# Due times of row tails, and half norms on VectorE, in a graph attention kernel

## The chip, the cores and the metric

The kernel runs on one core of one Trainium2 chip. The metric is the time of one execution on the device in microseconds (us). All times below are in microseconds unless marked otherwise. The engines are TensorE (PE in the profile; PEld is its weight load), VectorE (DVE), ScalarE (ACT), GpSimd (POOL) and SyncE (SP, which only issues transfers here). Each engine runs its own instructions in order and waits on semaphores for the others.

## The reference

Eight graphs (F) of 2048 nodes (N) with 256 channels (C) share one 0/1 adjacency matrix. Each gets masked attention with eight heads of 32 channels, a normalisation, a two-layer network, a second normalisation, and around the whole a residual and a third normalisation. All is float32.

```
qkv = einsum('fnc,ck->fnk', x, w_qkv)                  # q, k, v, 8 heads of 32
scores = einsum('fnhd,fmhd->fhnm', q, k) / sqrt(D)
scores = where(adj > 0, scores, -1e9)
t = einsum('fhnm,fmhd->fnhd', softmax(scores), v)
x1 = layernorm(x + t) * ln1_g + ln1_b
f_out = relu(x1 @ w1 + b1) @ w2 + b2
x2 = layernorm(x1 + f_out) * ln2_g + ln2_b
out = layernorm(x + x2)                                # no gain, no bias
```

`layernorm` subtracts the row's mean and divides by sqrt(variance + 1e-5).

## The kernel before

**Items.** `fast_path` walks 1024 items (f, qc, g, mb): graph f, chunk qc of 512 query rows (four a graph), group g of four heads (two), block mb of 128 keys (sixteen). So a chunk is 32 items and a graph 128. For one item `scores` issues the score matmuls of four heads into two PSUM pairs and two VectorE additions of the mask (L279) into a tile `p`; `exponentials` is one ScalarE activation over 128x2048 (L283); `values` multiplies with V and accumulates over the sixteen blocks (L310); `add_up` adds up the exponentials for the softmax denominators, some on GpSimd (L339), some by transfers that accumulate (L336). Scores run two items ahead of the values, and three PSUM pairs take turns. There are twelve `p` tiles. The very last half chunk (`ENDING`, the last chunk's second head group) is computed in two halves of 256 rows, with lines of its own (L264, L268, L298, L330, L332).

**Side work.** Everything else is written as generators: projections of the next graph (`project`, `ask`, `turn`), mask blocks, and for each chunk, when its 32 items are done, `denominator` (L383 to L398), `outcome` with `divide` (transposes, division by the denominators, and a transfer L418 that accumulates `x` into `y`), and `tail`. A tail is: `norm` of `y`; `feed_forward` (transposes of `y`, two layers on TensorE, GpSimd's scale L581 and shift L583 of the residual); `norm` again; GpSimd's scale L445 and shift L447; a transfer L450 that adds `x`; a third `norm`; the store L453. `norm` takes statistics on VectorE (L348, L349), computes 1/sqrt on GpSimd (L353 to L357) and applies it on ScalarE (L360). Each `yield n` hands back to the planner for n steps.

**The planner.** In every step `advance` first runs side work, then the step's exponential, scores and values are issued. Generators stand in a list sorted by their due time, the third argument of `start`; those that want a PSUM bank (`yield BANK`) go in that order as long as a budget of TensorE work a step (`credit`) lasts, or at once when one of them is due. A larger due time therefore puts a generator behind others. What the planner decides is fixed when the program is built; nothing is chosen at run time.

**Due times.** `outcome` starts a chunk's tail ten steps after its `begin`, due at `begin + 26`. Two chunks are special: chunk 1 of the last graph has `begin + 18` and two rows at a time (`per` 2), and chunk 2 of the last graph, which gets its residual from a tile `xb` through TensorE, starts at `begin + 4` and is due at `begin + 18`.

**The end.** The last chunk is finished by `closing(h)`, once for each half of 256 rows: five matmul terms of the denominators (L494) and their sum with the first head group's (L497), transposes, division (L526), residual (L529), statistics (`half_stats`, L460 to L464, 1/sqrt on GpSimd), `half_norm` (a small VectorE product L469 and two ScalarE activations L471), GpSimd's scale and shift L535 and L536, the two layers, and the two remaining norms with L559, L564 and L565 between them, then the store L569. When the items are out, `advance` runs what is left in the order of due times; half 1 has the earlier due time.

Of the kernel before, what the change touches and what calls it, by code (L numbers as in the profile page):

```python
# [61 lines left out]
def fast_path(ctx, tc, cst, x, adj, out, RS):  # L62
# [339 lines left out]
    def outcome(f, qc):  # L402
        yield ROOM
        state["tails"] += 1
        xin = x[f, qc * CH:(qc + 1) * CH, :].rearrange("(p j) c -> p j c", p=P)
        y = yp.tile([P, TPC, C], F32, name="y")
        begin = items.index((f, qc, 1, LAST)) + SUM + 2
        yield from divide(f, qc, y)
        if (f, qc) == (F - 1, NCK - 2):
            xb = state["xb"]  # L410
            for j in range(0, TPC, 2):
                yield BANK
                ps = bank()
                columns(ps, ident, xb[:, j:j + 2, :].rearrange("p j c -> p (j c)"), start=True, stop=True)
                nc.vector.tensor_tensor(y[:, j:j + 2, :], ps.rearrange("p (j c) -> p j c", c=C), y[:, j:j + 2, :], ALU.add)
            start(begin + 4, tail(f, qc, y, xin, 2, xb), begin + 18)
            return
        nc.gpsimd.dma_start(y, xin, accum_op=ALU.add)  # L418
        if (f, qc) == (F - 1, NCK - 3):
            start(begin + 10, tail(f, qc, y, xin, 2), begin + 18)  # L420
        else:
            start(begin + 10, tail(f, qc, y, xin), begin + 26)

    def divide(f, qc, y):
        rc = RC.pop((f, qc))
# [9 lines left out]
    def tail(f, qc, y, xin, per=1, xb=None):  # L435
        yield from norm(y, per)
        yield from feed_forward(y)
        if xb is not None:
            nc.gpsimd.tensor_tensor(xb, xb, rows(cst["be2r"]), ALU.add)
        yield 1  # L440
        z = y
        yield from norm(z, per if per == 1 else TPC)
        while xb is None and per > 1 and state["now"] % MB not in CALM:
            yield 1
        nc.gpsimd.tensor_tensor(z, z, rows(cst["g2r"]), ALU.mult)  # L445
        yield 1
        nc.gpsimd.tensor_tensor(z, z, rows(cst["be2r"]) if xb is None else xb, ALU.add)  # L447
        yield 1
        if xb is None:
            nc.gpsimd.dma_start(z, xin, accum_op=ALU.add)  # L450
            yield 7 if per == 1 else 10
        yield from norm(z, per)
        nc.sync.dma_start(out[f, qc * CH:(qc + 1) * CH, :].rearrange("(p j) c -> p j c", p=P), z)  # L453
        state["tails"] -= 1

    def half_stats(t):
        mv = small.tile([P, 2, nc.vector.BN_AGGR_DIM], F32, name="mv")
        for j in range(2):
            st = small.tile([P, nc.vector.BN_STATS_DIM], F32, name="st")
            nc.vector.bn_stats(st, t[:, j, :])  # L460
            nc.vector.bn_aggr(mv[:, j, :], st)
        rs = small.tile([P, 2], F32, name="rs")
        nc.gpsimd.tensor_scalar(rs, mv[:, :, 1], EPS, 1.0, op0=ALU.add, op1=ALU.mult)
        nc.gpsimd.tensor_tensor(rs, rs, cst["mhalf"][:, 0:2], ALU.pow)  # L464
        return mv, rs

    def half_norm(t, mv, rs):
        nb = small.tile([P, 2], F32, name="nb")
        nc.vector.scalar_tensor_tensor(nb, mv[:, :, 0], -1.0, rs, op0=ALU.mult, op1=ALU.mult)  # L469
        for j in range(2):  # L470
            nc.scalar.activation(t[:, j, :], t[:, j, :], AF.Identity, bias=nb[:, j:j + 1], scale=rs[:, j:j + 1])  # L471

    def closing(h):
        f, qc, g = ENDING
        own, part, t0 = slice(2 * h, 2 * h + 2), slice(h * HQ, (h + 1) * HQ), len(items) - MB // 2 * (2 - h)
        terms = [(5, 6), (1, 7), (0, 7), (6, 8), (7, 8)]
        dst = out[f, qc * CH + h * HQ:qc * CH + (h + 1) * HQ, :].rearrange("(p j) c -> p j c", p=P)

        def row2(v):
            return v[:, None, :].to_broadcast([P, 2, C])  # L480

        yield BANK
        ps = bank()
        for n, (block, when) in enumerate(terms):
            if n:
                yield MORE
            while state["now"] < t0 + when:
                yield WAIT
            term = PT.pop((*ENDING, block + h * MB // 2))
            state["credit"] -= 4 * CH  # L490
            for b in range(2):
                for i in range(4):
                    r = D * i
                    nc.tensor.matmul(ps[r:r + D, 0:HQ], cst["halves"][:, g, :], term[:, i, b * HQ:(b + 1) * HQ],  # L494
                                     start=(n + b == 0), stop=(n + b == len(terms)))
        dT = DT[f, qc]
        nc.vector.tensor_tensor(dT[:, part], ps[:, 0:HQ], dT[:, part], ALU.add)  # L497
        if h == 0:
            state["y"] = yp.tile([P, TPC, C], F32, name="y")
            state["ff"] = [work.tile([P, 2, CH], F32, name=n) for n in ("turned", "hT")]  # L500
        y, (yT, hT) = state["y"][:, own], state["ff"]
        xr, xb = (t[:, own] for t in state["rows"])
        def turned_sums():
            ps = bank()
            transposes(ps, [dT[:, part][:, j::2] for j in range(2)])
            den = ps[:, 0:HQ].rearrange("p (j c) -> p j c", c=P)[:, :, ::D // 2]
            rc = op.tile([P, 2, H], F32, name="rc")
            nc.vector.reciprocal(rc, den)
            return rc, den

        def count(den):
            nc.vector.tensor_tensor(RS[:, 0, own], RS[:, 0, own], den, ALU.add)
            nc.vector.tensor_tensor(RS[:, 1, own], RS[:, 1, own], den, ALU.min)

        yield 1
        if h == 0:
            yield BANK
            rc, den = turned_sums()
            count(den)
        yield BANK  # L520
        po = bank()
        transposes(po, [OT[f, qc, gg][:, part][:, j::2] for gg in range(2) for j in range(2)])
        if h:
            rc, den = turned_sums()
        for gg in range(2):
            nc.vector.tensor_tensor(y[:, :, gg * P:(gg + 1) * P].rearrange("p j (h d) -> p j h d", d=D),  # L526
                                    po[:, gg * HQ:(gg + 1) * HQ].rearrange("p (j h d) -> p j h d", h=4, d=D),
                                    rc[:, :, gg::2, None].to_broadcast([P, 2, 4, D]), ALU.mult)
        nc.vector.tensor_tensor(y, y, xr, ALU.add)  # L529
        found = half_stats(y)  # L530
        if h:
            count(den)
        yield 1
        half_norm(y, *found)
        nc.gpsimd.tensor_tensor(xr, y, row2(cst["g1r"]), ALU.mult)  # L535
        nc.gpsimd.tensor_tensor(xr, xr, row2(cst["be1b2r"]), ALU.add)  # L536
        yield BANK
        ps = bank()
        transposes(ps, [y[:, j, a * P:(a + 1) * P] for a in range(2) for j in range(2)])
        for a in range(2):  # L540
            nc.scalar.activation(yT[:, a, part], ps[:, a * HQ:(a + 1) * HQ], AF.Identity,
                                 bias=cst["be1c"][:, a:a + 1], scale=cst["g1c"][:, a:a + 1])
        yield 1
        for d in range(2):
            yield BANK
            ps = bank()
            for a in range(2):
                columns(ps[:, 0:HQ], w1s[:, a, d * P:(d + 1) * P], yT[:, a, part], start=(a == 0), stop=(a == 1))
            nc.scalar.activation(hT[:, d, part], ps[:, 0:HQ], AF.Relu, bias=cst["b1s"][:, d:d + 1], scale=1.0)
        yield 1  # L550
        yield BANK
        ps = bank()
        for j in range(2):
            if j:
                yield MORE
            for d in range(2):
                columns(ps[:, j * C:(j + 1) * C], hT[:, d, part][:, j * P:(j + 1) * P], w2s[:, d, :], start=(d == 0), stop=(d == 1))
        z = y
        nc.vector.tensor_tensor(z, ps.rearrange("p (b c) -> p b c", c=C), xr, ALU.add)  # L559
        found = half_stats(z)  # L560
        yield 1
        half_norm(z, *found)
        yield 1
        nc.vector.tensor_tensor(z, z, row2(cst["g2r"]), ALU.mult)  # L564
        nc.vector.tensor_tensor(z, z, xb, ALU.add)  # L565
        found = half_stats(z)
        yield 1
        half_norm(z, *found)
        nc.sync.dma_start(dst, z)  # L569
# [40 lines left out]
    def start(t, gen, due):  # L610
        fill.append([t, gen, 1, due])
        fill.sort(key=lambda e: e[3])
# [408 lines left out]
```

## Time and profile before

| what | value |
|---|---|
| median of three runs | 3159.01 (3158.67 to 3160.27) |
| the profiled execution | 3158.02 |
| its span, first to last instruction | 3156.0 |
| mean granted TensorE clock | 0.994 |
| first item to last scores of the loop | 53.2 to 3105.9 |
| each of graphs 2 to 6 | 379.9 |
| graph 0, graph 1 | 386.1, 382.6 |
| from the last scores to the end | 50.1 |

The span is counted from the first instruction to the last; some 2 us of the execution's time lie around it. The length of a graph is the distance between the first scores matmul of its first item and that of the next graph's. In views of the timeline a line gives start, length, engine, source line, operation, output and inputs, shape, count, and in brackets the engine's idle time before it and what ended it. VectorE instructions overlap a little, so the next one can begin some 0.08 before the one in front has ended in the records.

### The profile page before, as it was taken

What the parts mean: (1) busy time and instruction counts of PE and PEld (TensorE: products, weight loads), DVE (VectorE), ACT (ScalarE), POOL (GpSimd) and SP (SyncE); (2) the same over time, 40 slices, a digit from 0 to 9 for tenths busy, and PEclk for the clock granted to TensorE, in tenths of its full rate; (3) what the DMA queues carried; (4) which work ended last, traced back from release to release, by engine and by line L of the source; (5) the groups of instructions that cost most, each with busy time, mean ns of one, the idle gap of its engine ahead of it and who ended that gap; (6) DMA issues with size and microseconds to landing.
All of it is one profiled execution on the core that took longest, in us unless ns stands there. A gap on an engine that the chain in (4) does not pass through costs nothing.

```text
span 3156.0 us, 68508 instructions
## 1 busy us (share of the span) xinstructions
PE 3051.3 (97%) x28988; PEld 962.6 (31%) x28988; DVE 2747.6 (87%) x3139; ACT 2427.1 (77%) x1934; POOL 2727.7 (86%) x1389
## 2 busy tenths in 40 slices
PE   8999999999999999999999999999999999999986
PEld 4222333233332233223332323323333233322223
DVE  4989888998888988888988888988888988889885
ACT  4877878777778877778777878778778778778774
POOL 1768989888889888899888899899989899899985
PEclk9999999999999999999999999999999999999998
DMA  8998878889789888789878899788888889778871
GB/s 258 223 210 185 196 170 194 193 191 198 173 174 209 197 190 178 170 195 214 192 169 187 187 207 195 166 184 204 197 176 191 190 192 202 167 173 166 173 157 42
DMA packets 165465, 586.86 MB, mean 186 GB/s; under 512 B 15360, under 2 KB 84480, under 8 KB 116512
## 3 DMA queue, kind: packets, MB, share of 16 engines
q0 software_dynamic: 63696, 430.60, 69.4%
q1 hardware_dynamic: 100640, 150.50, 14.1%
q8 instruction: 229, 3.75, 0.5%
q10 hardware_dynamic: 816, 1.31, 0.1%
q14 instruction: 84, 0.69, 0.1%
HBM read 146.15 MB, written 37.75 MB: 58 GB/s over the span
## 4 chain that ended last, share of the span: by engine, by line


## 5 line engine op out<-in xcount | busy, mean ns | idle before, releaser
L279 DVE TENSOR_TENSOR p<-s,mask 128x1024 f32<-128x1024 f32 x2016 | 2371.5, 1218 | 297.7 <-PE s L276 123.4
L283 ACT ACTIVATE p<-p 128x2048 f32<-128x2048 f32 x1024 | 1955.7, 1910 | 551.1 <-DVE p L279 449.1
L339 POOL TENSOR_TENSOR p<-p 128x2048 f32<-128x2048 f32 x409 | 1999.9, 4890 | 221.3 <-ACT p L283 200.4
L276 PE MATMUL s<-qT,kT 32*128 32x512 f32 x8064 | 1152.0, 640 | 56.5 <-DVE p L279 52.6
L310 PE MATMUL x<-p,v 128*32 128x512 f32 x8064 | 1075.8, 606 | 5.8 <-ACT p L283 4.2
L276 PEld LDWEIGHTS s<-qT,kT 32*128 32x128 f32 x8064 | 315.3, 183 | 659.5 <-DVE p L279 629.4
L336 POOL DMA_DIRECT2D p<-p x378 | 416.2, 1104 | 49.2 <-ACT p L283 41.0
L310 PEld LDWEIGHTS x<-p,v 128*32 128x32 f32 x8064 | 158.7, 108 | 771.3 <-issue 315.1
L54 PE MATMUL x<-in,wqkv 128*32 128x512 f32 x1888 | 245.7, 592 | 0.0
L383 PE MATMUL x<-p,halves 128*32 128x512 f32 x1768 | 231.1, 594 | 1.6 <-DVE kT L170 1.4
L360 ACT ACTIVATE y<-y,nb,rs 128x256 f32<-128x256 f32 x372 | 218.3, 591 | 0.5 <-POOL nb L357 0.5
L348 DVE BATCH_NORM_STATS2 st<-y 128x6 f32<-128x256 f32 x372 | 154.8, 416 | 0.0
L54 PE MATMUL x<-turned,w1s 128*32 128x512 f32 (+1 forms) x1008 | 125.2, 593 | 0.0
L54 PEld LDWEIGHTS x<-wqkv,in 128*32 128x32 f32 x3584 | 102.4, 110 | 66.5 <-issue 55.4
L54 PE MATMUL x<-w2s,hT 128*32 128x256 f32 x2048 | 122.0, 379 | 0.0
L54 PE MATMUL x<-wqkv,in 128*32 128x128 f32 x3584 | 118.2, 273 | 0.0
L54 PEld LDWEIGHTS x<-in,wqkv 128*32 128x32 f32 x1888 | 61.3, 110 | 141.3 <-issue 116.0
L354 POOL TENSOR_TENSOR rs<-rs,mhalf 128x4 f32<-128x4 f32 x93 | 96.2, 1035 | 7.8
L445 POOL TENSOR_TENSOR y<-y,g2r 128x1024 f32<-128x1024 f32 x31 | 99.3, 3205 | 2.2 <-ACT y L360 2.2
L383 PEld LDWEIGHTS x<-p,halves 128*32 128x32 f32 x1768 | 57.3, 110 | 133.9 <-issue 126.5
L447 POOL TENSOR_TENSOR y<-y,be2r 128x1024 f32<-128x1024 f32 x30 | 94.4, 3145 | 0.2
L54 PEld LDWEIGHTS x<-w2s,hT 128*32 128x32 f32 x2048 | 66.4, 110 | 69.7 <-issue 35.6
(164 smaller groups left out, 1433.6 us busy)
## 6 DMA issues: line engine op xcount, KB each, us to landing
p<-p POOLq DMA_DIRECT2D x380, 1024.0 KB, 9.1
in<-xd SPq DMA_DIRECT2D x87, 512.0 KB, 7.5
mask<-md SPq DMA_DIRECT2D x248, 128.0 KB, 5.4
y<-in_x_dram POOLq DMA_DIRECT2D x60, 512.0 KB, 10.3
out_dram<-y SPq DMA_DIRECT2D x31, 512.0 KB, 4.5
in<-in_x_dram SPq DMA_DIRECT2D x30, 512.0 KB, 6.8
xd<-in SPq DMA_DIRECT2D x28, 512.0 KB, 6.8
p<-in_adj_dram SPq DMA_DIRECT2D x8, 1024.0 KB, 14.3
```

The source lines that it names most:

```text
L54: nc.tensor.matmul(out[r:r + D], lhsT[:, r:r + D], rhs, start=start, stop=stop)
L276: nc.tensor.matmul(ps2[half][:, j, :], KT[f, mb // TPC, g][r:r + D, (mb % TPC) * P:(mb % TPC + 1) * P], QT[f, qc, g][r:r + D, :], start=Tr ...
L279: nc.vector.tensor_tensor(pt[:, 2 * half:2 * half + 2, :], ps, MK[f, qc, mb // 2][:, mb % 2, None, :].to_broadcast([P, 2, CH]), ALU.add)
L283: nc.scalar.activation(PT[item], PT[item], AF.Exp, scale=1.0 / math.sqrt(D))
L310: nc.tensor.matmul(O[grp][r:r + D, :], V[f, mb // TPC, g][:, mb % TPC, r:r + D], PT[item][:, h, :], start=(mb == 0), stop=(mb == LAST))
L336: nc.gpsimd.dma_start(PT[f, qc, g, chain[0]], PT.pop(item), accum_op=ALU.add)
L339: nc.gpsimd.tensor_tensor(first, first, PT.pop(item), ALU.add)
L348: nc.vector.bn_stats(st, t[:, j, :])
L354: nc.gpsimd.tensor_tensor(rs, rs, cst["mhalf"], ALU.pow)
L360: nc.scalar.activation(t[:, j, :], t[:, j, :], AF.Identity, bias=nb[:, j:j + 1], scale=rs[:, j:j + 1])
L383: nc.tensor.matmul(ps[r:r + D, :], cst["halves"][:, g, :], term[:, h, :], start=(n == 0), stop=(n == len(blocks) - 1))
L445: nc.gpsimd.tensor_tensor(z, z, rows(cst["g2r"]), ALU.mult)
```

## The change

Four edits. The due time of the ordinary tails goes from `begin + 26` to `begin + 30`; that of chunk 2 of the last graph from `begin + 18` to `begin + 14`. In that chunk's tail the scale and the addition of `xb` are issued in one step, and the third norm's four rows in one step instead of two by two. In `closing`, `half_norm` becomes one VectorE instruction for each of its two row blocks, (t - mean) * rs, without L469 and ScalarE; GpSimd's scale and shift of the residual `xr` are issued after the transposes and their copies instead of before; and the second norm with gain and shift becomes two VectorE passes, (z - mean) * g2, which does not need 1/sqrt, and then * rs + xb.

```diff
@@ outcome
-            start(begin + 4, tail(f, qc, y, xin, 2, xb), begin + 18)
+            start(begin + 4, tail(f, qc, y, xin, 2, xb), begin + 14)
...
-            start(begin + 10, tail(f, qc, y, xin), begin + 26)
+            start(begin + 10, tail(f, qc, y, xin), begin + 30)
@@ tail
         nc.gpsimd.tensor_tensor(z, z, rows(cst["g2r"]), ALU.mult)
-        yield 1
+        if xb is None:
+            yield 1
         nc.gpsimd.tensor_tensor(z, z, rows(cst["be2r"]) if xb is None else xb, ALU.add)
...
-        yield from norm(z, per)
+        yield from norm(z, per if xb is None else TPC)
@@ half_norm
-        nb = small.tile([P, 2], F32, name="nb")
-        nc.vector.scalar_tensor_tensor(nb, mv[:, :, 0], -1.0, rs, op0=ALU.mult, op1=ALU.mult)
         for j in range(2):
-            nc.scalar.activation(t[:, j, :], t[:, j, :], AF.Identity, bias=nb[:, j:j + 1], scale=rs[:, j:j + 1])
+            nc.vector.tensor_scalar(t[:, j, :], t[:, j, :], mv[:, j, 0:1], rs[:, j:j + 1], op0=ALU.subtract, op1=ALU.mult)
@@ closing
         half_norm(y, *found)
-        nc.gpsimd.tensor_tensor(xr, y, row2(cst["g1r"]), ALU.mult)
-        nc.gpsimd.tensor_tensor(xr, xr, row2(cst["be1b2r"]), ALU.add)
         yield BANK
...
         yield 1
+        nc.gpsimd.tensor_tensor(xr, y, row2(cst["g1r"]), ALU.mult)
+        nc.gpsimd.tensor_tensor(xr, xr, row2(cst["be1b2r"]), ALU.add)
...
-        found = half_stats(z)
-        yield 1
-        half_norm(z, *found)
-        yield 1
-        nc.vector.tensor_tensor(z, z, row2(cst["g2r"]), ALU.mult)
-        nc.vector.tensor_tensor(z, z, xb, ALU.add)
+        mv, rs = half_stats(z)
+        for j in range(2):
+            nc.vector.scalar_tensor_tensor(z[:, j, :], z[:, j, :], mv[:, j, 0:1], cst["g2r"], op0=ALU.subtract, op1=ALU.mult)
+        yield 1
+        for j in range(2):
+            nc.vector.scalar_tensor_tensor(z[:, j, :], z[:, j, :], rs[:, j:j + 1], xb[:, j, :], op0=ALU.mult, op1=ALU.add)
         found = half_stats(z)
```

Both programs do the same matmuls. The lines of the changed kernel that the prediction names are L470 (the new `half_norm`), L561 and L564 (the two passes), L448 (GpSimd's addition in `tail`) and L496 (the sum of the denominators).

## The prediction

> **What bounds the kernel now.** First the page: shares of the engines, then TensorE and its clock by slice.
>
> ```profile
> span 3156.0 us, 68508 instructions
> ...
> PE 3051.3 (97%) x28988; PEld 962.6 (31%) x28988; DVE 2747.6 (87%) x3139; ACT 2427.1 (77%) x1934; POOL 2727.7 (86%) x1389
> ...
> PE   8999999999999999999999999999999999999986
> DVE  4989888998888988888988888988888988889885
> ```
>
> TensorE is busy everywhere but at the two ends, so work moved from step to step gains nothing unless it fills time in which TensorE waits. The view of stretches shows single steps; a step is the time from one item's first scores matmul to the next item's.
>
> ```profile
> 1588.43:1592.22 3.79, 3.79 (x52) 1.51 (x48) 2.36 (x2) 2.57 (x3) 3.79 (x3) 1.00 0.69 174
> 1640.28:1643.20 2.92, 2.92 (x28) 0.72 (x24) 2.85 (x5) 1.91 (x1) 2.91 (x2) 1.00 0.40 95
> 1666.63:1669.29 2.66, 2.66 (x25) 0.90 (x21) 2.16 (x3) 2.44 (x2) 2.49 (x3) 1.00 0.96 179
> 1724.25:1726.81 2.56, 2.14 (x21) 0.47 (x17) 1.98 (x3) 2.37 (x2) 2.56 (x1) 1.00 0.98 204
> 1607.84:1611.04 3.20, 2.86 (x21) 1.03 (x21) 3.17 (x8) 1.91 (x1) 3.20 (x1) 1.00 1.01 205
> ```
>
> The columns are stretch, its length, then busy time of PE, PEld, DVE, ACT and POOL. A step with two units of side work on TensorE (16 `w2s` groups) takes 3.79, with one unit 2.92, with four transposes 2.66, with none 2.56. A unit is thus 3.79 - 2.92 = 0.87, and an empty step would take 2.92 - 0.87 = 2.05 if TensorE set it; it wastes about 0.5. In the last row VectorE is full: four transposes cost 3.20. The timeline shows why:
>
> ```profile
> 1605.40 0.68 DVE L389 TENSOR_TENSOR dT<-x,dT 128x512 f32<-128x512 f32 x1
> 1606.00 0.42 DVE L348 BATCH_NORM_STATS2 st<-y 128x6 f32<-128x256 f32 x1
> 1606.45 0.18 DVE L349 BATCH_NORM_AGGREGATE mv<-st 128x2 f32<-128x6 f32 x1
> 1606.56 2.36 DVE L279 TENSOR_TENSOR p<-s,mask 128x1024 f32<-128x1024 f32 x2
> ```
>
> Between two mask additions (2.36) stand an addition of 0.60 and a statistics pair of 0.56, so VectorE needs 3.4 where TensorE needs 2.7, and the next scores wait for it. At the end of the kernel the timeline has a chain instead:
>
> ```profile
> 3117.75 0.43 DVE L497 TENSOR_TENSOR dT<-s,dT 128x256 f32<-128x256 f32 x1 [6.62 <-PE s L494]
> 3125.50 1.09 ACT L471 ACTIVATE y<-y,nb,rs 128x256 f32<-128x256 f32 x2 [11.69 <-DVE nb L469]
> 3128.50 1.08 ACT L471 ACTIVATE y<-y,nb,rs 128x256 f32<-128x256 f32 x2
> 3150.03 1.09 ACT L471 ACTIVATE y<-y,nb,rs 128x256 f32<-128x256 f32 x2 [0.19 <-DVE nb L469]
> ```
>
> The last denominators are summed by 3118.18, the two halves' first norms end at 3126.59 and 3129.58, the last norm at 3151.12; the store ends the span at 3156.
>
> **The change: tails due four steps later.** No instruction is added or taken away before the last 14 steps; the order in which the two programs issue shows what moves. A later due time puts a tail's matmuls behind projections and denominators. I sorted the 1011 steps before the two programs are level again by their side work on TensorE. In each of graphs 2 to 6: before 4 empty, 28 with transposes, 84 single, 12 double; after 1, 28, 91, 7, and one triple (twelve denominator matmuls). Before: 10.47 (the four empty steps, one is 2.80) + 84 x 2.93 + 12 x 3.79 = 302.1. After: 2.54 + 91 x 2.93 + 7 x 3.79 + 4.66 = 300.4. That is -1.7 a graph. In the same way graph 0 has four doubles fewer, three singles and an empty step more, -3.8 (its tails end in graph 1); graph 1 -0.5; graph 7 five empty steps and two doubles fewer, six singles and a triple more, +2.0. Sum -10.9.
>
> Against it stands VectorE's debt. Before, the three transposing steps at the four chunk borders of a graph take 9.10, 9.10, 8.57 and 8.24: the dear ones are those where a tail's statistics pairs run up to the very step that sums the denominators, as in the rows at 1605.40. With the tails two to three steps later this is so at all four: 4 x 9.10 - 35.0 = +1.4. A step behind them costs 0.2 more (2.86 for 2.65, as after the first two borders before), and transposes of `y` now meet statistics pairs, 0.15. So +1.75 a graph, 8.7 for five; by the same rows +0.6 in graph 0 and +0.9 in graph 1; in graph 7 step 991 has five norms on ScalarE in place of four with a step of 2.54, +0.5. Sum +10.7. The loop gains 10.9 - 10.7 = 0.2. Its bounds: no debt at all, -10.9, and debt twice as dear, +10.5. I take the middle because the pattern that I price is the very one that stands at 1605.40.
>
> Other queues: GpSimd's scale and shift of a tail move from beside the last sums of a half (5.33 us at 1732.75, behind two of them) into steps where it has no sum, which costs nothing; without that cover it is 6.3 a chunk, late for the denominators. Mask additions wait for buffers that denominators free later: the tightest pair is a GpSimd accumulation issued 3 steps before (5 before); it lands 11.6 after its exponential, and 12.0 are there. SP's stores and reloads shift by the same steps and nothing waits on them.
>
> **The change: the last 14 steps.** The tail of chunk 2 is due four steps earlier, so from step 1012 its matmuls go two units a step. To the last scores that is one triple and four doubles, +1.7 (3107.6 for 3105.9). But two of the closing terms then run before, so behind the last values stand 16 matmuls for 40 (4.50 us in the rows), 1.8; and four ScalarE norms (2.06) no longer precede the last exponential, 0.8. The denominators would be ready at 3116.1 for 3117.7. New is a wait: VectorE has the four statistics pairs of that tail ahead of the last sum, and they wait for GpSimd's shift, which I put at 3114.1 (sum, scale and shift of 4.6, 2.4 and 2.4 from 3104.7). They end at 3116.4, the sum at 3116.8 for 3118.18: **-1.35**.
>
> **The change: half norms on VectorE.** The trace has no such operation. TENSOR_SCALAR on SBUF data takes 0.69 for 1024 elements (L700), a two-tensor operation 0.69 for 512 (L529), so the changed kernel's L470 is between 0.22 and 0.42 for 256 and its L561 and L564 about 0.40; I take 0.22 and 0.40. After the sum VectorE runs the reciprocals, divisions, additions and statistics of both halves, 7.0 by the rows (0.26, 0.76, 0.69, 1.15 a half and 1.2 of small ones); then one half's norm at once, the other's 1.1 later, when GpSimd has its `rs`. Both are done 8.5 after the sum, where before it was 11.4. The first matmul of the block comes 9.8 after, for 12.3: **-2.5**. GpSimd's scale and shift (four of 1.27) now stand behind; `xr` is needed only 8 us later.
>
> Those matmuls are slow at first. The stretch view:
>
> ```profile
> 3130.00:3135.00 5.00, 5.00 (x47) 2.31 (x49) 0.00 (x0) 1.97 (x4) 3.81 (x6) 0.50 0.01 3
> 3136.00:3140.00 4.00, 4.00 (x78) 2.21 (x70) 1.44 (x4) 0.75 (x2) 0.00 (x0) 1.00 0.00 0
> ```
>
> The granted clock is 0.50 until some 6.4 us after TensorE's unbroken work begins at 3129.14. I keep that delay. The Trainium skill (TensorE: Matmul & The Clock Gate, "What's actually happening") gives about 3.4 us of busy time, which would make this stretch about 2 us shorter still.
>
> Behind the last matmul (3139.9) come 16.1 us. After: first sum, statistics, scaled difference (0.8), second sum, statistics, 0.8, then 0.8 and statistics for each half: 8.0 after the last matmul; `rs` 1.1, norm 0.45, issue 0.1, store 4.85: 14.5 to 15.0. I take 14.8: **-1.3**. This supposes that GpSimd's `rs` keeps its 0.19 and 0.70. It does not always:
>
> ```profile
> 3146.19 0.54 POOL L463 TENSOR_SCALAR rs<-mv 128x2 f32<-128x2 f32 x1 [2.91 <-DVE mv L461]
> 3146.82 1.15 POOL L464 TENSOR_TENSOR rs<-rs,mhalf 128x2 f32<-128x2 f32 x1
> ```
>
> There VectorE ran L564 and L565 with two SBUF inputs. The skill's GPSIMD Engine Reference (Specifications) says that GpSimd's SBUF interface is shared with VectorE, in contention with just such instructions and with its two-port modes, and the change makes more of both; by it the end would take 0.8 to 2.4 more.
>
> **Sum.** -0.2 - 1.35 - 2.5 - 1.3 = -5.4 against the profiled execution, 3158.02 (span 3156.0 and 2.0 around it): 3152.6. The median of the runs shown is 1.0 above it: 3153.6.
>
> **Rivals.**
> - *The empty steps are won whole.* VectorE's debt does not grow, the loop gives 10.9 and the end 5.2: 3143. For it: VectorE is busy 87%, TensorE's waits on it are 52.6 us by the list of waits. Against: the 3.20 step. Half of it gives 3148.
> - *The residual lands too late (slower).* The tail's first norm starts at a fixed step, but the chunk's division, and with it the load of `x` that accumulates into `y` (L418), now slips by three steps in one chunk of each graph from 1 on: 4 steps before the statistics that wait for it on VectorE, where it was 7; in graph 1 once 3. Mask additions are queued behind. Now 18.7 us lie between the issue at 1711.66 and those statistics at 1730.4; three steps of 2.9 fewer leave 10.0, and that decides: the load lands 5.6 to 11.5 after its issue, so TensorE loses up to 1.5 in each of seven graphs and, with four steps fewer, up to 4.4 once, 14 in all: 3154 + 14 = 3168. Against: it takes 6 us where the last big accumulation was issued 6 us before, 11 only close behind one, and in that chunk it will be some 7 behind.
> - *The end gains little.* GpSimd is later than 3114.1 and the statistics hold the last sum (1.35), or each `rs` takes 1.69 as in the two rows above instead of 0.89 (0.8 for each that the end waits for, three of them): 2 to 4 less, 3156 to 3158.
>
> **How the numbers follow.** Forecast (3150 to 3156): 0.53; empty steps won: 0.20; little at the end: 0.17; late residual: 0.10. 0.2% is 6.3 us, about what a measurement can tell here: below 3152.7 is faster, above 3165.3 slower. The forecast lies 0.9 above the border, so 0.23 of its 0.53 are faster; with 0.20 of the first rival, 0.43. Slower: 0.07 of the late residual. Same: 0.50. The range leaves out the far ends of the first and second rival: 3147 to 3161.
>
> **What would show it.** In graphs 2 to 6 a graph of 379.9 stays within 0.5; steps of 2.56 nearly vanish, and the three transposing steps are near 9.1 at all four borders. VectorE waits for L418's transfer nowhere. From the last scores to the last closing matmul 8.5 in place of 11.8; from the last sum of denominators to the last matmul 19.2 in place of 21.7; from there to the end 14.8. I am wrong if a graph comes out at 378 or at 382.

## The result and the profile after

The kernel after takes 3152.49 (14 runs, 3150.73 to 3154.98) where the kernel before takes 3159.22 (14 runs, 3156.55 to 3160.78): ratio 0.998 [0.9973, 0.9987], 6.7 us or 0.2% less. In a second set of runs the two stood at 3153.22 (11 runs) and 3159.06 (22 runs), 5.8 less, 0.9981 [0.9972, 0.999]. The predicted time was 3153.6.

The profiled execution of after took 3153.11, span 3151.1. From the page, the span, the engines' shares, and TensorE and its clock by slice:

```profile
span 3151.1 us, 68554 instructions
...
PE 3052.4 (97%) x28988; PEld 962.1 (31%) x28988; DVE 2749.7 (87%) x3145; ACT 2416.7 (77%) x1922; POOL 2727.1 (87%) x1389
...
PE   7989999999999999999999999999999999999987
...
DVE  4989988989889989889988988889988899989886
...
PEclk9999999999999999999999999999999999999998
```

The shares did not move. What moved is seen only stretch by stretch, so the table divides the spans of the two profiled executions at the same events. The last column is what the prediction gave for the stretch.

| stretch | before | after | difference | predicted |
|---|---|---|---|---|
| start to first scores | 53.19 | 56.44 | +3.25 | 0 |
| graph 0 | 386.08 | 381.77 | -4.31 | -3.2 |
| graph 1 | 382.58 | 382.49 | -0.09 | +0.4 |
| graphs 2 to 6, each | 379.94 | 379.91 | -0.03 | +0.05 |
| graph 7 to item 1012 | 347.42 | 349.68 | +2.26 | +2.5 |
| item 1012 to last scores | 36.95 | 38.66 | +1.71 | +1.7 |
| last scores to last sum of denominators | 12.28 | 9.67 | -2.61 | -3.05 |
| that sum to the last matmul | 21.86 | 19.94 | -1.92 | -2.5 |
| last matmul to the end | 15.93 | 12.91 | -3.02 | -1.3 |

Three of these stretches contain chance, which the other profiles below bring out. The start varied from 53.2 to 56.4 over the profiles, with the same code; it waits for the first loads. Items 37 and 38 of graph 0 took 10.4 to 12.2 in kernels with the same code there; without them graph 0 is 374.25 before and 371.29 after, -2.96. And from the sum to the last matmul, two runs whose code there is that of before took 20.29 and 20.32, not 21.86; the last section says why.

The rows that answer to the prediction's 3.20 step are the three transposing steps of a chunk border, now as dear at the third and fourth border as at the first two. The view of stretches of after (stretch, its length, busy time of PE, PEld, DVE, ACT and POOL, granted clock, DMA share, GB/s):

```profile
1800.47:1809.54 9.07, 8.48 (x65) 3.08 (x61) 9.00 (x16) 5.44 (x3) 8.34 (x6) 1.00 0.94 190
1890.46:1899.56 9.10, 8.48 (x65) 3.08 (x61) 9.03 (x16) 5.50 (x3) 8.39 (x7) 1.00 1.00 203
```

The same two borders before:

```profile
1794.85:1803.42 8.57, 8.33 (x65) 3.08 (x61) 8.54 (x14) 5.51 (x3) 7.24 (x7) 1.00 1.06 214
1892.47:1900.71 8.24, 8.24 (x64) 3.08 (x60) 8.24 (x12) 6.05 (x4) 8.04 (x5) 1.00 1.02 207
```

VectorE has 16 instructions in a border of after, where it had 14 and 12: the added ones are statistics and their aggregation. It is busy for all but 0.07 of the stretch, while TensorE idles 0.6. That is the debt.

At the end of the kernel the timeline of after shows what the prediction did not foresee (start, length, engine, line, operation, output and inputs, shape, count, and in brackets the idle time before it and what ended it):

```profile
3117.81 0.42 DVE L496 TENSOR_TENSOR dT<-x,dT 128x256 f32<-128x256 f32 x1 [0.20 <-PE x L493]
...
3124.88 0.70 DVE L470 TENSOR_SCALAR y<-y,mv,rs 128x256 f32<-128x256 f32 x2
3126.11 1.26 POOL L541 TENSOR_TENSOR in<-y,g1r 128x512 f32<-128x512 f32 x1
3126.18 2.69 DVE L470 TENSOR_SCALAR y<-y,mv,rs 128x256 f32<-128x256 f32 x2 [0.59 <-POOL rs L465]
3127.45 1.27 POOL L542 TENSOR_TENSOR in<-in,be1b2r 128x512 f32<-128x512 f32 x1
```

The first line is the last sum of denominators. Behind it one half's two norms take 0.70, the other's 2.69. The slow pair starts 0.07 behind GpSimd's scale L541, and ends at 3128.87, 0.15 behind GpSimd's shift L542 (3128.72): one norm for each of the two GpSimd instructions.

### The profile page after: what moved, and what is told of

Read it like the earlier page. It is cut to its first block, busy times and chain, and to the rows that moved or that the text cites. A ratio compares the mean times of both kernels' runs of the same rounds, so it can differ in the third digit from the quotient of the medians.

```text
span 3151.1 us, 68554 instructions
## 1 busy us (share of the span) xinstructions
PE 3052.4 (97%) x28988; PEld 962.1 (31%) x28988; DVE 2749.7 (87%) x3145; ACT 2416.7 (77%) x1922; POOL 2727.1 (87%) x1389
## 5 line engine op out<-in xcount | busy, mean ns | idle before, releaser
L283 ACT ACTIVATE p<-p 128x2048 f32<-128x2048 f32 x1024 | 1955.3, 1910 | 541.1 <-DVE p L279 390.3
L339 POOL TENSOR_TENSOR p<-p 128x2048 f32<-128x2048 f32 x409 | 1957.2, 4785 | 230.2 <-ACT p L283 225.8
L336 POOL DMA_DIRECT2D p<-p x378 | 383.2, 1017 | 66.8 <-ACT p L283 54.6
L348 DVE BATCH_NORM_STATS2 st<-y 128x6 f32<-128x256 f32 x372 | 154.8, 416 | 3.2 <-POOL y L448 3.2
L448 POOL TENSOR_TENSOR y<-y,be2r 128x1024 f32<-128x1024 f32 x30 | 80.0, 2666 | 1.1
```

The source lines that it names most:

```text
L283: nc.scalar.activation(PT[item], PT[item], AF.Exp, scale=1.0 / math.sqrt(D))
L336: nc.gpsimd.dma_start(PT[f, qc, g, chain[0]], PT.pop(item), accum_op=ALU.add)
L339: nc.gpsimd.tensor_tensor(first, first, PT.pop(item), ALU.add)
```

## The experiments

The lengths of graphs 2 to 6 repeat from graph to graph and from run to run, nearly always within 0.1 us, so the loop is read from one profile. Whole times vary by some 2 us, so they are used only where many runs stand behind them.

**Each edit alone.** The first three kernels start from before. The first has only this:

```diff
-            start(begin + 10, tail(f, qc, y, xin), begin + 26)
+            start(begin + 10, tail(f, qc, y, xin), begin + 30)
```

> The kernel before, with only the due time of the ordinary tails four steps later. Theory (what the steps lose in side work, VectorE's debt at the chunk borders takes back): measured from first scores to first scores, graphs 2 to 6 each within 0.1 us of before, graph 0 about 4.0 shorter, graph 1 within 0.3, graph 7 up to its step 1012 about 2.2 longer; the loop in all about 2 shorter, the end unchanged. Rival (the empty steps are won, the debt is small): graphs 2 to 6 each 1.7 shorter, the loop 10 shorter.

Measured: graphs 2 to 6 at 379.89 to 379.94, graph 1 382.48, graph 0 383.08 (3.0 shorter without items 37 and 38, for 4.0 expected), graph 7 to item 1012 350.35, 2.9 longer for 2.2 expected. So the loop is only 0.3 shorter, for 2 expected. The time was 3157.24 beside 3158.46 for one execution of before. The theory holds for a steady graph, which gains nothing.

The second kernel has only the edits of chunk 2's tail in the last graph:

```diff
-            start(begin + 4, tail(f, qc, y, xin, 2, xb), begin + 18)
+            start(begin + 4, tail(f, qc, y, xin, 2, xb), begin + 14)
...
-        yield from norm(z, per)
+        yield from norm(z, per if xb is None else TPC)
```

> The kernel before, with only the edits of the tail of chunk 2 of the last graph (due four steps earlier, one pause less ahead of the addition, last norm in one piece). Theory: from the scores of item 1012 to the last scores about 1.7 longer than before, from the last scores to the last sum of denominators 9.7 in place of 12.3, so 0.9 won; everything before item 1012 as before. Rival (the wait for GpSimd's shift takes back what is won): the sum comes 12 or more after the last scores, and this edit costs 1.5.

Measured: item 1012 to the last scores 38.66, +1.71; from there to the sum 9.39, -2.89; so 1.2 won, and besides 0.75 behind the last matmul (15.18 for 15.93). Everything before item 1012 is as before. The wait that the rival feared is small: in after the statistics (L348 from 3115.38 to 3117.6) and the last closing matmuls (to 3117.75) end within 0.2 of each other.

The third kernel has only the edits in `half_norm` and `closing`:

```diff
-            nc.scalar.activation(t[:, j, :], t[:, j, :], AF.Identity, bias=nb[:, j:j + 1], scale=rs[:, j:j + 1])
+            nc.vector.tensor_scalar(t[:, j, :], t[:, j, :], mv[:, j, 0:1], rs[:, j:j + 1], op0=ALU.subtract, op1=ALU.mult)
...
```

> The kernel before, with only the edits of the last half blocks (norms on VectorE, the two fused passes, GpSimd's scale and shift behind). Theory: the last sum of denominators stands where it stood, 12.3 after the last scores; from the sum to the last matmul 20 in place of 21.7, with the second half's two norms on VectorE at 2.7 for the pair in place of 0.7; from the last matmul to the end 13 to 14 in place of 16.1; 4 to 5 won in all. Rival (GpSimd's slower small operations eat the gain behind the last matmul): 15.5 or more from there to the end.

Measured: last scores to the sum 12.27; sum to the last matmul 20.69 for 20 expected, with 1.95 for the second half's pair of norms, not 2.7; from there to the end 14.74, so 1.2 won there, for 2 to 3 expected. The 4 to 5 in all that I expected did not come. The time was 3156.79 beside 3158.46. The two ends are not additive: 0.75 and 1.2 alone, 3.0 together. SyncE's queue in this kernel's timeline shows why:

```profile
3147.99 1.66 SPq L567 DMA_DIRECT2D out_dram<-y  x2
3148.55 0.74 DVE L469 TENSOR_SCALAR y<-y,mv,rs 128x256 f32<-128x256 f32 x2 [0.59 <-POOL rs L464]
3149.75 0.75 SPq L453 DMA_DIRECT2D out_dram<-y  x1
```

The last norm ends at 3149.29, 9.3 behind the last matmul as in after, but chunk 2's tail still has its own big store (L453) to issue behind the two halves' stores, and the span ends 5.4 after the last norm. In after that store is out long before, and 3.6 are enough.

**VectorE's debt.** The next two kernels take the statistics of the second norm away from every ordinary tail, in before and in after:

```diff
-        yield from norm(z, per if per == 1 else TPC)
+        yield from norm(z, per if per == 1 else TPC, cst["unit"] if per == 1 else None)
```

`norm` then uses the constant (mean 0, variance 1) in place of `mv` and issues neither L348 nor L349; pauses and all other instructions stay.

> The kernel before with VectorE's four statistics pairs of the second norm left out of every ordinary tail (a constant mean 0 and variance 1 stands in their place, so the output is not the reference's); every other instruction and every pause is kept. It is the base for the next run. Theory: the transposing steps at the four chunk borders fall from 9.10, 9.10, 8.57 and 8.24 to about 8.0 each, and graphs 2 to 6 are 2.2 shorter than before. Rival (statistics do not delay these steps): no change of a graph.

> The kernel after with the same statistics left out in the same way. Theory (the later due time wins 1.7 a graph on TensorE and VectorE's statistics, now up against the denominators at all four borders, take it back): without them graphs 2 to 6 are each 1.5 shorter than in the run before this one. Rival (an empty step is bound by something else, so filling it wins nothing): graphs 2 to 6 equal in both.

Measured without the statistics: a steady graph is 377.71 on the base of before (2.23 shorter; graph 4 alone 378.08) and 376.15 on that of after (3.76 shorter; graph 4 376.29), so the later due time now wins 1.56 a graph, for 1.5 expected. All four borders take 8.24 in both (the first expectation said 8.0). The fourth border of the kernel with the later due time and without statistics:

```profile
1875.05:1883.29 8.24, 8.24 (x65) 3.09 (x61) 8.24 (x12) 5.57 (x3) 7.54 (x7) 1.00 1.02 207
```

VectorE has 12 instructions for 16, and the stretch falls from 9.10 to TensorE's own 8.24. So both terms of the loop's sum are real: 1.56 a graph won on TensorE, and 3.76 - 2.23 = 1.53 more lost to the statistics. They cancel because the same edit causes both.

**Moving the debt away.** If the statistics cost only by their place, they can be put behind the border:

```diff
         if xb is not None:
             nc.gpsimd.tensor_tensor(xb, xb, rows(cst["be2r"]), ALU.add)
-        yield 1
+        yield 7 if per == 1 else 1
         z = y
```

> The kernel after with seven steps of pause in place of one between an ordinary tail's last addition and the statistics of its second norm, so that these fall behind the denominators and transposes of the chunk border; nothing is added or left out. Theory (VectorE's debt at the borders is what kept the later due time from winning): graphs 2 to 6 each 2.9 shorter than before, the loop in all 17 shorter, time about 3135 to 3138. Rival (the debt only moves to the steps where the statistics now stand): graphs 2 to 6 within 0.5 of 379.9.

Measured: 3321.51. I was wrong. The debt is gone from the borders as expected: the first two of the three steps take 2.74 or 2.75 at all four, and at the second border the three take 8.24. But at the others the third step takes 6.7 to 11.9, and graphs 2 to 6 take 401.6 to 406.6. Two lines of the list of waits (waiting engine and line, what it waits for: us in all, times, longest):

```profile
DVE y L431 <- DMA out_dram<-y: 123.1, 20, 9.1
...
DVE p L279 <- DMA p<-p: 42.8, 15, 4.3
```

There are two `y` tiles. With six steps more in a tail its store is issued too late, the next chunk's division (L431) waits for it up to 9.1 on VectorE, and the mask additions queue behind. They also wait for `p` tiles that the accumulating transfers free late. The kernel after has neither wait.

Then three steps were given back ahead of the third norm, and GpSimd's shift at the end was moved as in the run below:

```diff
-            yield 7 if per == 1 else 10
+            yield 4 if per == 1 else 10
```

> The run before this one with, besides, four steps in place of seven ahead of the third norm's statistics, and with GpSimd's scale and shift of the last two halves in one piece behind both first norms. Theory: graphs 2 to 6 each 3.3 shorter than before, the loop about 20 shorter, the end 1.0 to 2.0 better than after; 3129 to 3134 in all, 0.8 to 0.9% under before. Rival (a wait for a buffer that the held tail frees later, or for a store): a graph at 378 or more and 3142 or more in all.

Measured: 3281.65 (5 runs), ratio to before 1.0381 [1.0367, 1.0395], graphs at 395.8 to 396.9. L431 no longer waits for a store. The longest waits are now in GpSimd's queue:

```profile
1647.93 5.26 POOL L339 TENSOR_TENSOR p<-p 128x2048 f32<-128x2048 f32 x1
...
1653.28 0.19 POOL L353 TENSOR_SCALAR rs<-mv 128x4 f32<-128x4 f32 x1
...
1655.20 0.60 ACT L360 ACTIVATE y<-y,nb,rs 128x256 f32<-128x256 f32 x1 [5.74 <-POOL nb L357]
1655.46 0.93 POOL L336 DMA_DIRECT2D p<-p  x1 [0.30 <-issue]
1655.70 1.89 ACT L283 ACTIVATE p<-p 128x2048 f32<-128x2048 f32 x1
```

The small products of the third norm (L353) stand behind a sum of exponentials; ScalarE's norm waits 5.74 for them, and the exponential (L283) is queued behind that norm: one step of 9.7. ScalarE waited 92.1 in all for these products, 8.9 in after. That is not all. The list of waits has two more that after does not have:

```profile
DVE st L348 <- DMA y<-in_x_dram: 39.2, 17, 4.0
DVE p L279 <- DMA p<-p: 36.4, 13, 3.8
```

The first is the price of the three steps given back: the third norm's statistics now reach VectorE before the transfer that adds `x` (L450 in before) has landed. How the loss divides among the three waits was not tested. My account of the loop had TensorE, VectorE and ScalarE, and took the tile count, GpSimd's queue and the landing of transfers for free. So the statistics can be paid for neither at the borders nor, by these two moves, behind them; other moves were not tried.

**What holds VectorE at the end.** In the kernel after, GpSimd's scale and shift of both halves are made one piece of twice the width, issued when both halves have their first norm:

```diff
-        nc.gpsimd.tensor_tensor(xr, y, row2(cst["g1r"]), ALU.mult)
-        nc.gpsimd.tensor_tensor(xr, xr, row2(cst["be1b2r"]), ALU.add)
+        state["normed"] = state.get("normed", 0) + 1
+        if state["normed"] == 2:
+            xw = state["rows"][0]
+            nc.gpsimd.tensor_tensor(xw, state["y"], rows(cst["g1r"]), ALU.mult)
+            nc.gpsimd.tensor_tensor(xw, xw, rows(cst["be1b2r"]), ALU.add)
```

> The kernel after, with GpSimd's scale and shift of both halves done in one piece of twice the width once both halves have their first norm. Theory (VectorE's two norms of the second half each stand until GpSimd's instruction beside them ends): that pair takes 0.7 to 0.8 in place of 2.69, and the last matmul comes 1.0 to 2.0 sooner behind the last sum of denominators, 18 to 19 in place of 19.95; scale and shift still end before the first addition that reads them. Rival (the pair waits for its own statistics or its rs): 2.7 as before, 20 from sum to last matmul.

> The kernel after with GpSimd's scale and shift in one piece behind both first norms, timed. Theory: the second half's norms end 1.95 sooner behind the sum of denominators, and the last matmul 1.0 to 2.2 sooner, the larger figure where the clock is granted full in the window after next: 3150.3 to 3151.5 where the kernel after stands at 3152.5. Rival (the low clock ends at its own time and takes it all back): equal to the kernel after within 0.5.

> The kernel after once more, on the same chip as the other runs of this call, to set them against: 3152.5, and in its profile again 10.6 from the last sum of denominators to the end of the second half's first norm, 12.9 from the last matmul to the end.

In the single run and the timed one the pair fell to 0.74 and 0.73, and the second half's norm ends 8.68 and 8.69 behind the sum, for 10.63 and 10.64 in the two profiles of after. The timeline of the timed run:

```profile
3122.35 0.70 DVE L470 TENSOR_SCALAR y<-y,mv,rs 128x256 f32<-128x256 f32 x2
...
3123.65 0.73 DVE L470 TENSOR_SCALAR y<-y,mv,rs 128x256 f32<-128x256 f32 x2 [0.59 <-POOL rs L465]
...
3124.47 2.37 POOL L544 TENSOR_TENSOR in<-y,g1r 128x1024 f32<-128x1024 f32 x1 [0.85 <-DVE y L470]
```

Same instruction, same wait for its `rs`; only GpSimd's instruction beside it is gone. The last matmul comes 17.76 and 17.28 behind the sum, for 19.94 and 20.33: 2.2 to 3.0 sooner, more than the 1.95, because the low clock also ends a window earlier (last section). Time: 3148.67 (6 runs, 3147.74 to 3151.62), ratio to before 0.9969 [0.9957, 0.9981], against 3153.22 and 0.9981 [0.9972, 0.999] for after on the same chip. This version beats both kernels: five of its six runs lie below the fastest of after's eleven (3150.93). Its gain over after, 4.5, exceeds the 1.0 to 2.2 that I expected; the profiles account for 2.2 to 3.0 of it; chance at the start may be the rest, which no run shows.

The other way to free the norm of GpSimd is to leave it on ScalarE, with all other edits kept:

```diff
-            nc.vector.tensor_scalar(t[:, j, :], t[:, j, :], mv[:, j, 0:1], rs[:, j:j + 1], op0=ALU.subtract, op1=ALU.mult)
+            nc.scalar.activation(t[:, j, :], t[:, j, :], AF.Identity, bias=nb[:, j:j + 1], scale=rs[:, j:j + 1])
```

> The kernel after with the norms of the last half blocks on ScalarE as before; order, fused passes and GpSimd's scale and shift behind both are kept. Theory (only VectorE's norm is held by GpSimd's instruction beside it, ScalarE's is not): the second half's pair takes 1.1 in place of 2.69, and ends 9.2 to 9.7 behind the last sum of denominators, where it is 10.6 after and 8.7 with scale and shift in one piece; behind the last matmul 0.6 to 0.9 more than after. Rival (the pair is late by its statistics or its rs): 10.5 or more.

Measured: 3153.40 (one run). The pair takes 1.08, as expected, but ends 10.90 behind the sum, the rival's number by neither of the rival's causes. The timeline:

```profile
3125.06 0.16 DVE L470 SCALAR_TENSOR_TENSOR nb<-mv,rs 128x2 f32<-128x2 f32 x1 [1.05 <-POOL rs L465]
...
3126.13 1.02 ACT L540 ACTIVATE turned<-s,be1c,g1c 128x256 f32<-128x256 f32 x2 [0.99 <-PE s L95]
3126.56 1.26 POOL L544 TENSOR_TENSOR in<-in,be1b2r 128x512 f32<-128x512 f32 x1
3127.04 1.08 ACT L472 ACTIVATE y<-y,nb,rs 128x256 f32<-128x256 f32 x2
```

`nb` is there at 3125.22, but ahead of the norm in ScalarE's queue stand the copies of the first half's transposes (L540), which wait for TensorE. That is also what the kernel before did at this place. Beside GpSimd's L544 the pair takes the 1.08 that it took in before, so ScalarE's norm is not held, as the theory says. So VectorE's norm does jump a queue, and in after GpSimd's pair takes nearly all of it back: 10.64 for 10.90. Behind the last matmul this run took 14.16, 1.25 more than after, for 0.6 to 0.9 expected: 0.48 until the last norm has ended and 0.77 from there.

**The due time against the ends.** The kernel after with `begin + 26` back:

> The kernel after with the ordinary tails' due time put back, so the kernel before with both edits at the end. Theory (the loop gains only some 0.7 from the due time, graph 0's gain of 3.0 being spent in graph 7): graphs 2 to 6 at 379.93, graph 0 3.0 longer than after, graph 7 up to step 1012 2.5 shorter; from the last scores to the end 41.6 to 42.5 as after; time 0.2 to 1.5 above the kernel after. Rival (the later due time is what made the kernel faster): within 1.5 of the kernel before.

Measured: 3154.82 (11 runs, 3150.33 to 3156.11), ratio to before 0.9984 [0.9975, 0.9993], 1.6 above after on the same chip, slightly more than expected, and 4.2 below before, so the rival falls; graphs 2 to 6 at 379.95, graph 7 to item 1012 347.44, last scores to the end 42.7. The intervals of the two kernels overlap, so the times alone do not tell them apart; the profiles give the due time 0.7 (-2.96 in graph 0, -0.1, five times -0.03, and in graph 7 +2.3 to +2.9 over the six profiles with the later due time, 2.5 on average).

## Why the prediction was right, and where it was wrong

- **The loop, -0.2: right.** -0.7 in the profiles (-0.3 to -1.0). The classes of steps and VectorE's debt were both sized to some 0.2 a graph: borders of 9.10, 9.18, 9.07 and 9.10 where "9.1 at all four" stood. Without the statistics the edit wins 1.56 a graph, so the rival of the empty steps falls by the debt and not by chance.
- **The rival of the residual that lands too late: fell.** No row has VectorE waiting for L418's transfer; it landed 5.4 to 11.2 after its issue, 6.9 in the middle.
- **The last 14 steps, -1.35: right.** +1.71 to the last scores as worked out, then -2.6 in after's profile and -2.9 in others: -0.9 to -1.2 in all. The new wait is there, within 0.3 of its place. The sum did not have a wait of TensorE in after's profile, 0.78 for a transfer that adds up exponentials (L332); the last sum came after TensorE's last term, and not after the statistics.
- **"Both are done 8.5 after the sum ... -2.5": wrong.** This is the step that failed. The first half's norms end 7.35 behind the sum, the second's 10.64, and the first matmul of the block comes 11.5 behind it, for 9.8 predicted and 12.3 before. One norm was put at 0.22 and takes 0.41, which is small. What failed is the overlap: GpSimd's scale and shift were said to "stand behind", and nothing was charged for the second half's norms running beside L541 and L542. I weighed a shared interface only for the small `rs` products behind the last matmul, where the runs show little (0.26 to 0.33 and 0.74 to 0.82, for 0.19 and 0.70). With GpSimd's work moved, the norms end at 8.7 and the block begins at 9.6, so the size was right for a kernel that was not built.
- **What that left of the -2.5.** Two pairs of profiles have nearly the same phase of the clock. In the first, the kernel with only the due time changed took 20.32 from the sum to the last matmul and after took 19.94; the block began 0.76 earlier, but the full clock came 14.2 behind the sum in both, so half of it was left, 0.4. In the second, the run with before's norms and chunk 2's tail moved took 20.52, and after's code 20.25 and 20.33.
- **The clock delay of 6.4 that I kept: wrong.** It was 3.5 in after's profile (3128.93 to 3132.46). The 6.4 of before's profile was its own phase of the clock: against the two other runs with that code (20.29 and 20.32) it is some 1.5 of the 1.9 by which this stretch is shorter. The prediction's other figure, 3.4, was nearer, but 3.0 less at half the clock makes 1.5, not the 2 that it gives.
- **Behind the last matmul, -1.3: mis-sized.** -3.0. The last norm ends 9.3 behind the last matmul, where the sum had 9.5 and before stood 11.1. The rest is the store: 4.85 was kept, and 3.6 was measured. About half of that is chunk 2's store, which no longer shares the end: with it gone and the norms still on ScalarE, 4.2 and 4.4 were measured. I had moved that tail four steps without moving its store in the sum. The other half came with the norms on VectorE; why is not shown.

So the total is right partly by luck: the store's 1.25, which was missed, made up for more than half of the 2.1 that the norms did not bring. With the chance at the start, in items 37 and 38 and in the clock's phase taken out, the stretches add up to -4.8 to -5.3, for -5.4 forecast. The medians show -6.7 and -5.8; where the rest lies, the profiles do not show.

## What to carry to other kernels

An edit that fills one engine's idle steps has to be costed on every engine that the moved work passes: here TensorE's gain and VectorE's loss were the same size, and both attempts to move the loss away ran into a tile count, GpSimd's queue and transfers that had not landed, at many times the price. Before a small operation on the path is moved from ScalarE to VectorE, look at what GpSimd runs at that very moment, and put GpSimd's long instructions behind it. In a short stretch after a pause, compare kernels at the same phase of the clock's windows, or over many runs.

## What the runs showed of the hardware

**VectorE and GpSimd.** Two VectorE instructions of 0.4 each took 1.35 and 1.42 beside two GpSimd instructions of 1.27, and each ended 0.15 behind one of them, in all five profiles with after's code there; in the three with GpSimd's pair behind both norms they took 0.41 each. In the kernel with only the end's edits of `half_norm` and `closing`, the first norm began 0.8 later beside GpSimd's scale, and again ended 0.15 behind it:

```profile
3127.40 1.26 POOL L540 TENSOR_TENSOR in<-y,g1r 128x512 f32<-128x512 f32 x1
3128.20 0.61 DVE L469 TENSOR_SCALAR y<-y,mv,rs 128x256 f32<-128x256 f32 x1
```

The Trainium skill (SBUF — State Buffer, section "SBUF: two separate sides") has the rule: the port pair is an exclusive lock that the first of the two engines holds for its whole instruction. It has it for VectorE instructions with two SBUF inputs or in a two-port mode; the norm has one such input, and no row names its mode. All nine profiles agree with a lock: a slowing by a shared rate would not end the instructions at the same distance behind GpSimd's, whenever they began.

**The clock.** The granted clock changes at the borders of windows of 3.41. The three low windows of after, with the one ahead of them and the one behind:

```profile
3118.81:3122.22 3.41, 0.71 (x6) 0.51 (x5) 3.21 (x13) 2.07 (x4) 0.83 (x5) 1.00 0.00 0
3122.22:3125.63 3.41, 0.31 (x1) 0.18 (x1) 3.30 (x13) 0.00 (x0) 1.15 (x3) 0.50 0.38 154
3125.63:3129.05 3.42, 1.48 (x6) 0.81 (x6) 2.69 (x2) 1.02 (x2) 3.11 (x4) 0.50 0.00 0
3129.05:3132.46 3.41, 3.41 (x31) 1.71 (x35) 0.00 (x0) 1.49 (x3) 2.44 (x2) 0.50 0.00 0
3132.46:3135.87 3.41, 3.41 (x72) 1.88 (x68) 0.00 (x0) 1.42 (x3) 0.00 (x0) 1.00 0.02 5
```

A window in which TensorE is busy for 0.71 is followed by half the clock here, and one in which it is busy throughout by the full clock. Before, a window of 2.94 busy was not followed by the full clock:

```profile
3128.69:3132.10 3.41, 2.94 (x20) 1.48 (x24) 0.00 (x0) 1.91 (x4) 2.95 (x3) 0.50 0.00 0
3132.10:3135.51 3.41, 3.41 (x36) 1.58 (x32) 0.00 (x0) 0.95 (x2) 1.79 (x5) 0.50 0.02 5
```

With the shift moved behind both norms, one of 3.23 was, after two low windows instead of three:

```profile
3123.12:3126.54 3.42, 3.23 (x20) 1.78 (x23) 0.73 (x2) 2.04 (x4) 2.57 (x2) 0.50 0.00 0
3126.54:3129.95 3.41, 3.41 (x68) 1.93 (x64) 0.00 (x0) 1.77 (x4) 2.68 (x2) 1.00 0.02 5
```

But in the first kernel that moved the debt away (3321.51), one of only 2.86 was too:

```profile
3297.25:3300.66 3.41, 2.86 (x23) 1.50 (x27) 0.49 (x1) 1.05 (x3) 2.88 (x3) 0.50 0.00 0
3300.66:3304.07 3.41, 3.41 (x68) 1.91 (x64) 0.00 (x0) 1.88 (x4) 0.00 (x0) 1.00 0.02 5
```

So busy time as the profile counts it does not decide alone, and these runs give no border. The windows stand at a different place in each execution, so the same code took 20.3 or 21.9 from the sum to the last matmul. The Trainium skill (TensorE: Matmul & The Clock Gate, section "What's actually happening") has the window of 3413 ns, free-running, and these windows agree; what counts as busy stays open here.
